# A state-space layer with its feed-forward part: y of a half in the bank of the side work, a third bank for A dt, fixed places for pieces of side work

## The chip, the cores and the metric

The kernel runs on one core of one Trainium2 chip. The metric is device time in microseconds (us) of one execution. The core's engines appear in the profile as PE (TensorE's matmuls), PEld (its weight loads), DVE (VectorE), ACT (ScalarE), POOL (GpSimd) and SP (SyncE, which issues the DMAs). Matmul results land in PSUM, a memory of eight banks of 512 f32 for each of 128 partitions.

## The reference, cut to what matters

```python
xn = x * rsqrt(mean(x * x) + 1e-6) * norm_w
xn = xn * sigmoid((xn @ select_proj_w.T + select_proj_b) * select_gate)
xp = xn @ x_proj_w.T                       # delta, B, C: 128 columns each
dt = softplus(delta @ dt_proj_w.T + dt_proj_b)
...
h = exp(dt[:, :, None] * A) * h + (dt * xt)[:, :, None] * bt[:, None, :]
y = einsum('bdn,bn->bd', h, ct)
...
x = layernorm(x + (y + x * D_param) @ out_proj_w.T)
x = layernorm(x + (silu(x @ w_gate.T) * (x @ w_up.T)) @ w_down.T)
```

There are 2 sequences of 1024 tokens, 512 channels, 128 states for each channel, and a hidden layer of 2048. All is f32.

## The kernel before

**Steps, halves, groups.** The tokens are taken in 64 *steps* of 32 tokens. A step has two *halves* of 256 channels, and a half has eight *groups* of 32 channels; so there are 1024 groups, numbered `k`, and `r = k % 8` is the place of a group in its half. For each group TensorE makes two matmuls `bu` (L705: dt x B, a tile of two banks) and two matmuls `a` (L417: A dt) for the *next* group. They use 32 rows of the array each, on four different row tiles, and are issued as bu, a, bu, a. ScalarE takes `exp` of the two `a` (L424) into `a_sb`, and VectorE runs the recurrence over the 32 tokens of the group with one scan (L726). The carried state enters at a group's first token: where the group is the first of a pair, VectorE adds it (L723), in every second group ScalarE copies it in (L713).

**y.** When a half's eight scans are done, `y_round` (L436) contracts its states with C: eight rounds of four matmuls, one round for four tokens. They run during the next half, as `ROUNDS` says: three behind group 1, three behind group 4, two behind group 7. Both halves of a step share one PSUM tile in a pool of its own (`ps_y`), and `y_out` (L449 to L452) empties it once a step: a ScalarE copy and three GpSimd operations.

**Side work.** Everything else is put between the groups by the class `Work`: `pre` (the projections of the next 256 tokens), `post` (out projection and first layer norm of 128 tokens) and `ffn`. These are Python generators. "E" asks for another engine's step (given at the top of every group by `others`), "P" begins a *piece* of TensorE work in the one bank of the pool `ps_m` (`misc`), "H" goes on with it. I call what runs between two yields a *unit*: two matmuls of 128 columns, or one of 256 columns. A piece of `gu` (gate and up), of `d` (down) or of `op` has 8 units, `sel`, `xp` and `ss` have 4, `zT`, `x1T`, `uT`, `z` have 2. A piece that has ended is emptied at the top of the next group: `gu`, `x1T` and the pieces of `pre` by ScalarE, `d` (L580), `op` (L487) and `zT` (L474) by VectorE. Until then `ps_m` holds it. `PARTS` gives credit for units behind each group: 4, 3, 3, 3, 3 behind groups 0, 2, 3, 5, 6, which is 16 in a half, and unused credit is kept up to 6.

**PSUM.** ps_y 1 bank, ps_m 1, ps_bu 2 x 2, ps_a 2: all eight. After the loop ps_bu and ps_a are released, the side work gets six banks more, and what is left of it runs alone.

Of the kernel before, what the change touches and what calls it, by code (L numbers as in the profile page):

```python
# [9 lines left out]
FP = mybir.dt.float32  # L10
# [5 lines left out]
P = 128  # L16
# [3 lines left out]

ROUNDS = ((), (0, 1, 2), (), (), (3, 4, 5), (), (), (6, 7))
PARTS = (4, 0, 3, 3, 0, 3, 3, 0)
RMS_EPS = 1e-6
# [11 lines left out]
def kernel(  # L35
# [122 lines left out]
    def misc(name):  # L158
        return bank_pool[0].tile([P, 512], FP, tag="m", name=name)
# [5 lines left out]
    def pre(c):  # L165
# [47 lines left out]
        for a in (slice(0, 2), slice(2, 4)):  # L213
# [3 lines left out]
            yield "E"  # L217
        yield "P"


        for m in range(NM):
            ps = misc(f"sel_{c}_{m}")
            yield from matmuls(ps, sel_w, m, xn)
            nc.scalar.activation(
                u[:, m, :], ps[:, 0:n], AF.Relu,
                bias=neg[:, 1, m : m + 1], scale=neg[:, 0, m : m + 1],
            )
            nc.scalar.activation(
                dt[:, m, :], ps[:, 0:n], AF.Abs, bias=gate_b[:, m : m + 1], scale=col(V_GATE, m)
            )  # L230
            yield "P" if m + 1 < NM else "E"
# [6 lines left out]
        yield "P"  # L238


        for g, dst in ((0, low), (2, c_sb)):
            ps = misc(f"xp_{c}_{g}")
            yield from matmuls(ps, xp_w, g, xn)
            nc.scalar.copy(dst, ps[:, 0:n])
            yield "P"

# [10 lines left out]
        for st in range(n_s):  # L257
# [4 lines left out]
            )  # L262
        yield "P"

        for a in range(0, NM, 2):
            ps = misc(f"z_{c}_{a}")
            for m in (a, a + 1):
                nc.tensor.matmul(  # L268
                    ps[:, ts(m - a, n)], dt_w[:, ts(m, P)], low, start=True, stop=True
                )  # L270
                yield "H" if m == a else "E"
            for m in (a, a + 1):
                z = ps[:, ts(m - a, n)]
                nc.scalar.activation(u[:, m, :], z, AF.Relu, bias=col(V_DTB, m))
                nc.scalar.activation(dt[:, m, :], z, AF.Abs, bias=col(V_DTB, m))
            yield "P" if a == 0 else "E"
        yield from softplus(dt, u)
# [4 lines left out]
        for j in range(n_j):  # L282
            yield "P"
            ps = misc(f"uT_{c}_{j}")
# [15 lines left out]
            if c == 0:  # L300
                load(0)
                diag(0, 0)
                diag(0, 1)
        yield "P"
        ps = misc(f"t0_{c}")
# [122 lines left out]
    def y_round(h, b):  # L428


        st, i = divmod(h, 2)
        if i == 0 and b == 0:
            ys[st] = ps_y.tile([P, 512], FP, tag="y", name=f"y_{st}")
        at = 28 + 28 * b
        for m in range(NM):
            nc.tensor.matmul(  # L436
                ys[st][ts(m, 32), ts(i, 256)], cz[st % 3][:, at : at + 32],
                hs[h][:, ts(m, 64), ts(b, 4)],
                start=(i == 0 and b == 0), stop=(i == 1 and b == 7),
                skip_group_check=True,  # L440
            )

    def y_out(st):

        tt, s = divmod(st, 4)
        if s == 0:
# [3 lines left out]
        nc.gpsimd.tensor_tensor(yc, yc, pick.unsqueeze(1).to_broadcast([P, P, 4]), ALU.mult)  # L450
        nc.gpsimd.tensor_tensor(yc[:, :, 0:2], yc[:, :, 0:2], yc[:, :, 2:4], ALU.add)
        nc.gpsimd.tensor_tensor(yrs[tt][:, s, :], yc[:, :, 0], yc[:, :, 1], ALU.add)  # L452
        if s == 3:
            work.add(post(tt), front=True)
# [3 lines left out]
    def post(tt):  # L458
# [6 lines left out]
        yield "E"  # L465
        yield "P"
        ps = misc(f"zT_{tt}")
# [10 lines left out]
        nc.sync.dma_start(x1, xf[tt])  # L478
        yield "P"
        ps = misc(f"op_{tt}")  # L480
# [22 lines left out]
    def ffn(tt, row):  # L503
# [24 lines left out]
        x1T = ffn_pool.tile([P, NM, P], FP, tag="x1T", name=f"x1T_{tt}")  # L528
        yield "P"
        ps = misc(f"x1T_{tt}")  # L530
# [7 lines left out]
        for what in order:  # L538
            part = int(what[1])
            if what[0] == "g":  # L540
# [3 lines left out]
                for f in range(0, NH, 2):  # L544
                    fetch(at + 4)
                    yield "P"
                    ps = misc(f"gu_{tt}_{part}_{f}")
# [20 lines left out]
            for half in range(2):  # L568
                fetch(at + 4)
                yield "P"  # L570
                ps = misc(f"d_{tt}_{part}_{half}")
# [48 lines left out]
    class Work:  # L620


        def __init__(self):
            self.gens, self.holder = [], None

# [17 lines left out]

        def tensor(self):

            if self.holder is not None:
                if self.holder[1] != "H":
                    return False
                self.step(self.holder)
                return True  # L650
            for item in self.gens:
                if item[1] == "P":
                    self.holder = item
                    self.step(item)
                    return True
            return False

        def finish(self, item):
# [21 lines left out]
    pres, begun, credit = {}, set(), 0  # L680
# [74 lines left out]
    y_out(NS - 1)  # L755
    ps_a.release()
# [8 lines left out]

    for pool in (bank_pool[0], ps_m, ps_y, hid_pool[0], ffn_pool, post_pool, main):
        pool.release()
# [67 lines left out]
```

## Time and profile before

| | |
|---|---|
| three runs | 2877.86, 2883.38 (median), 2885.7 us |
| profiled execution | 2885.05 us, span of its instructions 2882.4 us |
| first scan begins, last scan ends | 43.3 us, 2795.9 us |
| DVE busy | 2460.8 us, of which 1024 scans of 2283 ns: 2326.7 us |
| ACT busy | 1640.0 us, of which 2048 exp of 582 ns: 1084.8 us |
| POOL busy | 1838.5 us |
| granted TensorE clock, mean | 0.985 |

Busy times are sums over the whole span; a matmul row is as long as the profiler models it, and four matmuls on four row tiles can run at once, so that PE's busy time is a union and not a sum. "Idle before" names what ended an engine's idle time. The loop over the groups is nearly the whole span: it is followed by a tail of 87 us.

### The profile page before, as it was taken

Reading aid. Unit: us, or ns where it says so; the run is one execution under the profiler, and the core shown is the slowest. Engines: PE = TensorE matmul, PEld = TensorE weight load, DVE = VectorE, ACT = ScalarE, POOL = GpSimd, SP = SyncE. Lnnn points to the kernel's source line nnn. Section 1 sums busy time; section 2 is a strip of 40 time slices with the busy share of each in tenths; the row PEclk is TensorE's granted clock in tenths of the full one; section 3 lists DMA queues with packets and bytes.
Section 4 is the critical chain, followed back from the end, with each engine's and each line's share of the span. In section 5 each row is a group of like instructions: output and inputs, shape, how many; then the busy total and the mean of one; then the engine's idle time right before and its main releaser. Section 6 shows DMA issues by size and latency. Waiting matters only on the chain.

```text
span 2882.4 us, 58142 instructions
## 1 busy us (share of the span) xinstructions
PE 2781.4 (96%) x22728; PEld 1518.3 (53%) x22728; DVE 2460.8 (85%) x1680; ACT 1640.0 (57%) x3663; POOL 1838.5 (64%) x2140
## 2 busy tenths in 40 slices
PE   7989899999999999999999999999999999999998
PEld 4434454555555555455555555555555555555558
DVE  3998789899998988898998988889998899889970
ACT  4656556555665556555666556655566555555543
POOL 4666576666666666666666666566666666666643
PEclk6999999999999999999999999999999999999999
DMA  2012221324223231223312332222331332333337
GB/s 75 20 34 74 88 89 63 96 73 136 82 76 105 89 122 52 85 96 103 105 56 82 114 103 100 67 91 83 118 100 55 111 100 96 112 102 107 103 107 234
DMA packets 139166, 266.86 MB, mean 93 GB/s; under 512 B 22480, under 2 KB 76240, under 8 KB 138896
## 3 DMA queue, kind: packets, MB, share of 16 engines
q1 hardware_dynamic: 138896, 263.16, 28.5%
q8 instruction: 182, 2.98, 0.4%
q14 instruction: 88, 0.72, 0.1%
HBM read 250.39 MB, written 12.71 MB: 91 GB/s over the span
## 4 chain that ended last, share of the span: by engine, by line
PE 84%; DVE 7%; issue 3%; ACT 3%; POOL 1%; DMA 1%; SPq 0%; DVEq 0%; ACTq 0%; POOLq 0%
PE bu L705 30%; PE gu L552 17%; PE y L436 15%; PE d L574 7%; PE a L417 7%; DVE h L726 6%; PE sel L186 2%; PE op L483 2%; PE xp L186 1%; ACT a_sb L424 1%; DMA ub_d<-uT 1%; PE b L250 1%; PE ss L203 0%; PE z L268 0%; SPq L296 0%
## 5 line engine op out<-in xcount | busy, mean ns | idle before, releaser
L726 DVE TENSOR_TENSOR_SCAN h<-a_sb,bu 128x1024 f32<-128x1024 f32 x1024 | 2326.7, 2283 | 267.1 <-ACT bu L713 144.4
L424 ACT ACTIVATE a_sb<-a 128x496 f32<-128x496 f32 x2048 | 1084.8, 582 | 445.5 <-PE a L417 370.1
L417 PE MATMUL a<-ddt,a_t 32*128 32x512 f32 x4096 | 1275.7, 647 | 7.5 <-ACT a_sb L424 4.7
L705 PE MATMUL bu<-du,ub 32*128 32x512 f32 x4096 | 1224.8, 646 | 28.1 <-DVE h L726 22.7
L388 POOL TENSOR_TENSOR ddt<-dt,hot 128x512 f32<-128x512 f32 x512 | 532.8, 1048 | 291.5 <-PE a L417 291.5
L552 PEld LDWEIGHTS gu<-x1T,w 128*128 128x128 f32 x4096 | 481.9, 192 | 231.1 <-issue 175.2
L398 POOL TENSOR_TENSOR du<-ub,hot 128x512 f32<-128x512 f32 x512 | 534.8, 1048 | 38.9 <-PE a L417 35.2
L552 PE MATMUL gu<-x1T,w 128*128 128x128 f32 x4096 | 536.8, 283 | 11.0 <-ACT x1T L536 3.5
L705 PEld LDWEIGHTS bu<-du,ub 32*128 32x128 f32 x4096 | 351.5, 184 | 354.3 <-issue 209.5
L436 PE MATMUL y<-h,cz 128*32 128x256 f32 x8192 | 523.3, 384 | 1.2 <-DVE h L726 1.2
L436 PEld LDWEIGHTS y<-h,cz 128*32 128x32 f32 x8192 | 227.3, 109 | 403.2 <-issue 291.0
L713 ACT COPY bu<-cu 128x32 f32<-128x32 f32 x496 | 94.1, 190 | 578.0 <-PE a L417 514.5
L417 PEld LDWEIGHTS a<-ddt,a_t 32*128 32x128 f32 x4096 | 393.0, 185 | 47.7 <-ACT a_sb L424 28.8
L592 POOL TENSOR_SCALAR gu<-gu 128x256 f32<-128x256 f32 x128 | 108.2, 845 | 294.0 <-ACT gu L560 289.6
L574 PE MATMUL d<-w,hid 128*128 128x256 f32 x1024 | 257.1, 393 | 7.9 <-ACT t L314 3.0
L574 PEld LDWEIGHTS d<-w,hid 128*128 128x128 f32 x1024 | 184.2, 190 | 126.9 <-issue 81.6
L450 POOL TENSOR_TENSOR yc<-yc,pick 128x512 f32<-128x512 f32 x64 | 66.5, 1039 | 153.7 <-ACT yc L449 153.7
L723 DVE TENSOR_TENSOR bu<-bu,cd 128x32 f32<-128x32 f32 x496 | 92.9, 187 | 74.0 <-PE a L417 69.1
L600 POOL TENSOR_TENSOR hid<-gu,e 128x256 f32<-128x256 f32 x128 | 93.1, 728 | 65.5 <-ACT e L598 64.7
L374 POOL TENSOR_TENSOR cd<-cd,h 128x256 f32<-128x256 f32 x124 | 106.3, 857 | 39.9 <-DVE h L726 39.9
L560 ACT COPY gu<-gu 128x512 f32<-128x512 f32 x128 | 75.0, 586 | 60.3 <-PE gu L552 60.1
L593 POOL TENSOR_TENSOR gu<-gu 128x256 f32<-128x256 f32 x128 | 94.2, 736 | 10.7
(89 smaller groups left out, 1384.0 us busy)
## 6 DMA issues: line engine op xcount, KB each, us to landing
w<-in_wgu_s_dram SPq DMA_DIRECT2D x256, 512.0 KB, 4.8
w<-in_wd_s_dram SPq DMA_DIRECT2D x128, 512.0 KB, 3.8
cd<-dt_d SPq DMA_DIRECT2D x62, 256.0 KB, 3.4
ub<-ub_d SPq DMA_DIRECT2D x64, 128.0 KB, 2.0
cu<-ub_d SPq DMA_DIRECT2D x124, 64.0 KB, 4.8
ub_d<-bt SPq DMA_DIRECT2D x64, 64.0 KB, 1.7
ub_d<-uT SPq DMA_DIRECT2D x64, 64.0 KB, 1.8
zT<-in_x_q_dram SPq DMA_DIRECT2D x16, 256.0 KB
```

What stands on the lines that cost most here:

```text
L374: nc.gpsimd.tensor_tensor(cd, cd, last, ALU.mult)
L388: nc.gpsimd.tensor_tensor(ddts[j][:, m, :, :], made[lot_of[st]][0][:, a + m, toks(st)].unsqueeze(1).to_broadcast([P, 16, S]), hot[:, ts(i, ...
L398: nc.gpsimd.tensor_tensor(dus[j][:, m, :, :], uv[:, a + m, :].unsqueeze(2).to_broadcast([P, 16, S]), hot.unsqueeze(1).to_broadcast([P, 16, ...
L417: nc.tensor.matmul(ps, a_t[ts(g, 32), m, :], ddts[k // 4][ts(g, 32), m % 2, :, :], start=True, stop=True,)
L424: nc.scalar.activation(a_sb[:, k % 3, ts(b, 16), 1:], ps[:, :, 1:], AF.Exp, scale=-1.0)
L436: nc.tensor.matmul(ys[st][ts(m, 32), ts(i, 256)], cz[st % 3][:, at : at + 32], hs[h][:, ts(m, 64), ts(b, 4)], start=(i == 0 and b == 0), s ...
L552: nc.tensor.matmul(ps[:, ts(2 * a + b, P)], w[:, a, k, :], x1T[:, k, :], start=(k == 0), stop=(k == NM - 1),)
L574: nc.tensor.matmul(ps[:, 0:HD], hid[:, f, :], w[:, f % 4, :], start=(f == 0), stop=(f == NH - 1),)
L592: nc.gpsimd.tensor_scalar_max(g, g, -80.0)
L593: nc.gpsimd.tensor_tensor(gu[:, 1, :], g, gu[:, 1, :], ALU.mult)
L705: nc.tensor.matmul(bu[:, ts(b, 16), :], prepared[st][ts(g, 32), 1, :], dus[k // 4][ts(g, 32), m % 2, :, :], start=True, stop=True,)
L726: nc.vector.tensor_tensor_scan(hs[h][:, ts(r, 32), :].rearrange("p q t -> p (q t)"), a_sb[:, k % 3, :, :].rearrange("p q t -> p (q t)"), b ...
```

## The change

```diff
-ROUNDS = ((), (0, 1, 2), (), (), (3, 4, 5), (), (), (6, 7))
-PARTS = (4, 0, 3, 3, 0, 3, 3, 0)
+ROUNDS = ((), (), (0, 1, 2, 3), (4, 5, 6, 7), (), (), (), ())
+PARTS = (4, 4, 0, 0, 3, 3, 4, 4)
+ROOM = (8, 4, 0, 0, 8, 4, 4, 8)
...
-    ps_y = tc.alloc_tile_pool(name="ps_y", bufs=1, space=PSUM)
...
-        yield "P"
+        yield NM
...
         nc.gpsimd.tensor_tensor(cd, a_n, cd, ALU.mult)
-        nc.scalar.activation(cd, cd, AF.Exp, scale=-1.0)
+    def carry_exp(st):
+        if st % NSB:
+            nc.scalar.activation(carried[st][0], carried[st][0], AF.Exp, scale=-1.0)
...
-        if i == 0 and b == 0:
-            ys[st] = ps_y.tile([P, 512], FP, tag="y", name=f"y_{st}")
+        if b == 0:
+            ys[h] = misc(f"y_{h}")
...
-        yc = post_pool.tile([P, P, 4], FP, tag="yc", name=f"yc_{st}")
-        nc.scalar.copy(yc, ys.pop(st).rearrange("p (q t) -> p q t", t=4))
+        yc = post_pool.tile([P, 64, 4], FP, tag="yc", name=f"yc_{h}", bufs=2)
+        nc.scalar.copy(yc, ys.pop(h)[:, 0:256].rearrange("p (q t) -> p q t", t=4))
...
-        def tensor(self):
+        def tensor(self, room=64):
             if self.holder is not None:
                 if self.holder[1] != "H":
                     return False
+                self.left -= 1
                 self.step(self.holder)
                 return True
             for item in self.gens:
-                if item[1] == "P":
-                    self.holder = item
+                if item[1] != "E" and item[1] <= room:
+                    self.holder, self.left = item, item[1] - 1
                     self.step(item)
                     return True
             return False
+        def idle(self):
+            while self.holder is not None:
+                self.others()
+                if self.holder is not None:
+                    self.tensor()
...
-    ps_a = tc.alloc_tile_pool(name="ps_a", bufs=2, space=PSUM)
+    ps_a = tc.alloc_tile_pool(name="ps_a", bufs=3, space=PSUM)
...
         work.others()
+        if r == 4 and h:
+            y_out(h - 1)
...
-            if i == 1 and st:
-                y_out(st - 1)
...
-        if h:
+        if ROUNDS[r] and h:
+            if r == 2:
+                work.idle()
             for b in ROUNDS[r]:
                 y_round(h - 1, b)
-        credit = min(credit + PARTS[r], 6)
-        for _ in range(min(credit, 4) if PARTS[r] else 0):
-            if not work.tensor():
-                break
-            credit -= 1
+        done = 0
+        while (done < PARTS[r] or done < 4 and work.left == 1) and work.tensor(ROOM[r] - done):
+            done += 1
...
         if r == 5 and i == 0 and st + 1 < NS:
             carry_a(st + 1)
+        if r == 7 and i == 0 and st + 1 < NS:
+            carry_exp(st + 1)
+    work.idle()
```

A half's y now lies in the bank of the side work (256 columns of it): four rounds behind group 2, four behind group 3, emptied at the top of group 4, for each half on its own. The bank that this frees goes to `a`. "P" becomes a number, the units of the piece that is to begin (the other places where it stood are changed in the same way), and `ROOM` says how large a piece may begin behind which group: 8 units behind groups 0, 4 and 7, up to 4 behind 1, 5 and 6, none behind 2 and 3, where y runs. There is no credit any more. The exp of `cd`, which carries a state into the next step, moves from group 5 to group 7. ScalarE's copy of every second group's first state (L713) stays as it is.

More of the change, by code (lines that the diff above doesn't have):

```diff
@@ L217, in pre @@
             yield "E"
-        yield "P"
+        yield NM
         for m in range(NM):
@@ L230, in pre @@
             )
-            yield "P" if m + 1 < NM else "E"
+            yield NM if m + 1 < NM else "E"
         yield from softplus(dt, u)
@@ L237, in pre @@
             yield "E"
-        yield "P"
+        yield NM
         for g, dst in ((0, low), (2, c_sb)):
@@ L244, in pre @@
             nc.scalar.copy(dst, ps[:, 0:n])
-            yield "P"
+            yield NM if g == 0 else n_j
         ps = misc(f"b_{c}")
@@ L262, in pre @@
             )
-        yield "P"
+        yield 2
         for a in range(0, NM, 2):
@@ L275, in pre @@
                 nc.scalar.activation(dt[:, m, :], z, AF.Abs, bias=col(V_DTB, m))
-            yield "P" if a == 0 else "E"
+            yield 2 if a == 0 else "E"
         yield from softplus(dt, u)
@@ L282, in pre @@
         for j in range(n_j):
-            yield "P"
+            yield 2
             ps = misc(f"uT_{c}_{j}")
@@ L303, in pre @@
                 diag(0, 1)
-        yield "P"
+        yield 1
         ps = misc(f"t0_{c}")
@@ L428, in y_round @@
     def y_round(h, b):
-        st, i = divmod(h, 2)
-        if i == 0 and b == 0:
-            ys[st] = ps_y.tile([P, 512], FP, tag="y", name=f"y_{st}")
+        if b == 0:
+            ys[h] = misc(f"y_{h}")
         at = 28 + 28 * b
@@ L436, in y_round, with y_out @@
             nc.tensor.matmul(
-                ys[st][ts(m, 32), ts(i, 256)], cz[st % 3][:, at : at + 32],
+                ys[h][ts(m, 32), 0:256], cz[h // 2 % 3][:, at : at + 32],
                 hs[h][:, ts(m, 64), ts(b, 4)],
-                start=(i == 0 and b == 0), stop=(i == 1 and b == 7),
+                start=(b == 0), stop=(b == 7),
                 skip_group_check=True,
             )
-    def y_out(st):
+    def y_out(h):
+        st, i = divmod(h, 2)
         tt, s = divmod(st, 4)
-        if s == 0:
+        if s == 0 and i == 0:
             yrs[tt] = post_pool.tile([P, 4, P], FP, tag="yr", name=f"yr_{tt}")
-        yc = post_pool.tile([P, P, 4], FP, tag="yc", name=f"yc_{st}")
-        nc.scalar.copy(yc, ys.pop(st).rearrange("p (q t) -> p q t", t=4))
-        nc.gpsimd.tensor_tensor(yc, yc, pick.unsqueeze(1).to_broadcast([P, P, 4]), ALU.mult)
+        yc = post_pool.tile([P, 64, 4], FP, tag="yc", name=f"yc_{h}", bufs=2)
+        nc.scalar.copy(yc, ys.pop(h)[:, 0:256].rearrange("p (q t) -> p q t", t=4))
+        nc.gpsimd.tensor_tensor(yc, yc, pick.unsqueeze(1).to_broadcast([P, 64, 4]), ALU.mult)
         nc.gpsimd.tensor_tensor(yc[:, :, 0:2], yc[:, :, 0:2], yc[:, :, 2:4], ALU.add)
-        nc.gpsimd.tensor_tensor(yrs[tt][:, s, :], yc[:, :, 0], yc[:, :, 1], ALU.add)
-        if s == 3:
+        nc.gpsimd.tensor_tensor(yrs[tt][:, s, ts(i, 64)], yc[:, :, 0], yc[:, :, 1], ALU.add)
+        if s == 3 and i == 1:
             work.add(post(tt), front=True)
@@ L465, in post @@
         yield "E"
-        yield "P"
+        yield 2
         ps = misc(f"zT_{tt}")
@@ L478, in post @@
         nc.sync.dma_start(x1, xf[tt])
-        yield "P"
+        yield 2 * NM
         ps = misc(f"op_{tt}")
@@ L528, in ffn @@
         x1T = ffn_pool.tile([P, NM, P], FP, tag="x1T", name=f"x1T_{tt}")
-        yield "P"
+        yield 2
         ps = misc(f"x1T_{tt}")
@@ L545, in ffn @@
                     fetch(at + 4)
-                    yield "P"
+                    yield 2 * NM
                     ps = misc(f"gu_{tt}_{part}_{f}")
@@ L569, in ffn @@
                 fetch(at + 4)
-                yield "P"
+                yield NH
                 ps = misc(f"d_{tt}_{part}_{half}")
@@ L623, in __init__ @@
         def __init__(self):
-            self.gens, self.holder = [], None
+            self.gens, self.holder, self.left = [], None, 0
         def add(self, gen, front=False):
@@ L675 @@
     ps_bu = tc.alloc_tile_pool(name="ps_bu", bufs=2, space=PSUM)
-    ps_a = tc.alloc_tile_pool(name="ps_a", bufs=2, space=PSUM)
+    ps_a = tc.alloc_tile_pool(name="ps_a", bufs=3, space=PSUM)
     for b in range(2):
         decay_exp(0, b, decay_mm(0, b))
-    pres, begun, credit = {}, set(), 0
+    pres, begun = {}, set()
     for k in range(NG):
@@ L752 @@
             carry_a(st + 1)
+        if r == 7 and i == 0 and st + 1 < NS:
+            carry_exp(st + 1)
+    work.idle()
     for j in range(8):
         y_round(2 * NS - 1, j)
-    y_out(NS - 1)
+    y_out(2 * NS - 1)
     ps_a.release()
@@ L764 @@
         work.tensor()
-    for pool in (bank_pool[0], ps_m, ps_y, hid_pool[0], ffn_pool, post_pool, main):
+    for pool in (bank_pool[0], ps_m, hid_pool[0], ffn_pool, post_pool, main):
         pool.release()
```

## The prediction

> **What bounds the kernel now.** I read the page's busy shares first, then the chain of waits, then single groups in the timeline, then the list of waits.
>
> ```profile
> PE 2781.4 (96%) x22728; PEld 1518.3 (53%) x22728; DVE 2460.8 (85%) x1680; ACT 1640.0 (57%) x3663; POOL 1838.5 (64%) x2140
> PE 84%; DVE 7%; issue 3%; ACT 3%; POOL 1%; DMA 1%; SPq 0%; DVEq 0%; ACTq 0%; POOLq 0%
> ```
>
> TensorE carries the end: 84% of the chain, and busy 96%. VectorE follows close, 85%. The Trainium skill (page "Trainium Kernel Development and Optimization", Performance Expectations) says that matmul busy time is a bad metric, because matmuls are pipelined. By the row, 2882.4 - 2781.4 = 101 us is all that any new order can win. The timeline sides with the rule. Two groups (start us, length, engine, line, what; bu and a alternate):
>
> ```profile
> 1404.07 0.59 PE L705 MATMUL bu<-du,ub 32*128 32x512 f32 x1
> 1404.61 2.05 PE L552 MATMUL gu<-x1T,w 128*128 128x128 f32 x16
> 1404.90 1.05 ACT L424 ACTIVATE a_sb<-a 128x496 f32<-128x496 f32 x2
> 1406.59 0.69 PE L705 MATMUL bu<-du,ub 32*128 32x512 f32 x1
> ...
> 1416.82 0.69 PE L705 MATMUL bu<-du,ub 32*128 32x512 f32 x1
> 1417.22 0.69 PE L417 MATMUL a<-ddt,a_t 32*128 32x512 f32 x1
> 1418.27 0.71 PE L552 MATMUL gu<-x1T,w 128*128 128x128 f32 x4
> ```
>
> The group at 1403.54 has its four matmuls side by side and is done with them at 1404.61: 1.07 us. In the group at 1416.82 the last `a` begins only at 1417.22, and the side work at 1418.27, after 1.45 us. TensorE counts as busy all the while. What the late `a` waited for:
>
> ```profile
> PEld bu L705 <- DVE h L726: 42.9, 40, 1.7
> PEld a L417 <- ACT a_sb L424: 28.8, 81, 2.8
> PEld op L483 <- DVE zT L474: 13.9, 11, 1.6
> PEld d L574 <- DVE x L580: 10.0, 10, 1.4
> PEld gu L552 <- DVE x L580: 6.6, 7, 1.4
> ```
>
> The exp of the `a` before it, in the same bank. The row's 28.8 us counts only empty queues. So I compared, for every group, the end of both exps with the start of the block behind them: in some 280 of 1020 blocks an exp ends too late, and these blocks lose 161 us together, 21 of it in the first 64 groups. There the scan sets the pace (157.9 us for 64 groups, and 64 x 2.283 + 24 x 0.187 = 151 us are DVE's own), so 140 us can be had.
>
> **TensorE's own time.** Two rounds of y take 1.00 us (1415.82 to 1416.82), three 1.43 (1407.66 to 1409.09): 0.43 a round. Four units of gu take 1.98, three 1.53: 0.45 a unit. A block of bu and a takes 1.08, and whatever follows it some 0.18 once. From the order of both programs I count the units behind each group. The loop before: 2552 us by these prices, of 2752 (40.2 to 2792.2). The loop after holds 48 units more, since the tail falls from 164 to 116, but more groups have nothing behind them (151 against 55), each of which saves 0.18: 2557 us. **+5.**
>
> **A third bank for a.** Each `a` then waits for an exp one earlier. At today's exp times the 140 us would shrink to about 41. But the groups become less even. The commonest half has 4, 0, 0, 0, 3, 3, 2, 4 units, and 81 of 128 groups r = 1 are empty (75 behind the start). There the next block comes 1.11 us after its predecessor. The exps of a block with ScalarE's copy end their first at 1.89 (start 1403.54; two exps from 1404.90 to 1405.95). The second `a` of r = 2 needs just that one: it waits 1.89 - 1.11 = 0.78, say 0.8 us. The bounds: nothing, if PE is held up elsewhere; 0.97, which short blocks behind an empty group lose today on two banks. 75 x 0.8 = 60 us. I keep 20 for waits behind late ScalarE steps, half of the remaining 41. 140 becomes 80: **-60.** The scan doesn't stop PE there: bu of r = 2 needs the buffer of r = 0, whose scan ends 1.74 + 2.29 = 4.03 us after that group began, and PE arrives at 3.05 + 1.11 = 4.16. Elsewhere 36 groups behind the start are empty, two in a row as a rule, and there PE does wait for scans (about 2.0 us for a pair by the same reckoning, 36 us in all). Today's 25 such groups lose some 16 us by the same cause: **+20.**
>
> **y in the bank of the side work.** Against this change speaks a rule of the Trainium skill ("Perfetto Trace Analysis", Matmuls): independent matmul groups should rotate through different PSUM banks, so that the evacuation of one overlaps the next one's matmuls. Here y joins a queue for one bank. By the rule each of 127 halves pays two evacuations, 0.58 before y and 0.37 behind it (rows of 512 and 256 columns): 120 us. By the rows nearly none is seen: a bank filled behind one group is emptied at the top of the next, and there PE has 1.08 us of bu and a in front of its next use. The cover fails where VectorE empties it, since its scan of 2.28 us is ahead in the queue. At 1451.64 zT ends the work of its group, its addition starts at 1454.09, and op at 1454.80, 0.8 us after its block. In the order of before 36 pieces emptied by VectorE have the next user behind the very next group; after, 73: 15 zT to op, 37 d to the next piece, 21 to y. The three rows above hold 30.5 us in 28 waits, 1.09 each. For the 52 I take the same share and price, 52 x 28/36 x 1.09 = 44, for the 21 in front of y (behind two blocks of PE work) 0.3: 50 us in all, **+20.** Between zero and the longest wait shown, 1.6 us for all 73 (+86).
>
> **Other edits.** y_out: ScalarE copies 128 x 0.37 instead of 64 x 0.58, +10 us; GpSimd 128 x (0.73 + 0.46 + 0.3) against 64 x 2.07, +58 us (the rows of 256 and 128 columns; the last is an estimate from them). They lie beside TensorE's groups; ScalarE is 57% and GpSimd 64% busy. Behind the copy in ScalarE's queue wait the next exps, but y has ended by the time they become possible. Behind GpSimd's wait stand `ddt` and `du`, wanted two groups later, 5 us. Without that cover each would cost 0.4 us a half, 50 us. cd's exp two groups later has its result due a half later: nothing. SP's queue gets no new DMA. Side work of the next 256 tokens was once forced (one group of 13.2 us, 8 over its price); the new order has none: -8. But uT and t now follow in adjacent groups for all lots, and ScalarE waits for their DMAs (13.1 us in t's row today); some 1 us a lot: +8. Together **0.**
>
> **The tail.** Before, 2792.2 to 2882.4 us: 90.2. Its first part did what was left of token block 14, and the chain of the last block (y, out projection, layer norm) lay beside that:
>
> ```profile
> 2795.93 3.64 PE L436 MATMUL y<-h,cz 128*32 128x256 f32 x58 [1.18 <-DVE h L726]
> 2804.51 3.72 PE L483 MATMUL op<-out_w,zT 128*128 128x256 f32 x16 [0.85 <-DVE zT L474]
> 2808.06 14.45 PE L552 MATMUL gu<-x1T,w 128*128 128x128 f32 x128
> 2810.86 0.81 ACT L499 ACTIVATE x<-x,off_a,rstd_a 128x512 f32<-128x512 f32 x1 [0.40 <-POOL off_a L498]
> ```
>
> After, only one d is left over. The chain stands alone: from the last bu d 4.8 us, its emptying 0.6, y 3.5, yc 2.1, zT and the addition 1.7, op 3.8, layer norm 3.6: 20.1. From x1T of the last block to the end are 52.9 us today (2829.5 to 2882.4). 20.1 + 52.9 = 73: **-17.**
>
> **Sum.** +5 - 60 + 20 + 20 + 0 - 17 = -32. The profiled execution took 2885.05 us (2.65 around its span), 1.7 above the median of 2883.38. 2885 - 32 = **2853.**
>
> **Rivals.**
> 1. *The third bank does more*: PE, held up earlier in the half by another wait, reaches r = 2 later and finds its bank free, as 1.89 - 1.11 needs only 0.8 us of delay. Both remainders (60 + 20) fall away: 2773; with half, 2813. For it speaks that VectorE's queue is seldom empty; against it, that delay of PE costs the same. I put it at 2795.
> 2. *One bank becomes the stall*: each of the 73 neighbours costs the longest wait shown, 1.6 us: 117 - 30.5 = +86 instead of +20, so 2919. It decides from (50 + 32) / 73 = 1.1 us for each. For it: behind these pieces PE runs ahead of a scan that takes 2.28 us; against it: 8 of 36 such places show no wait today.
> 3. *Nothing comes of it*: where no late exp holds PE, the scan does (1023 scans and their additions need 2430 us of the loop), and the wait only changes its name: -60 becomes about -30, 2883. That the third bank isn't used is no case: three tiles rotate by construction.
>
> **Numbers.** Forecast 0.45, own range 2830 to 2876; rival 1 0.17, rival 2 0.24, rival 3 0.14. Runs of this kernel tell 0.3%, 9 us, from no change. Faster: the forecast but for its upper edge (0.43) and rival 1: 0.60. Within: rival 3's middle and that edge, 0.13. Slower: rival 2 and the rest of rival 3, 0.27. The range 2800 to 2908 leaves out the far half of rival 2 and the lower end of rival 1.
>
> **What would show it.** Right: the wait of `a` on `a_sb` survives only behind empty groups, mostly at r = 2; the last scan ends near 2781; the tail is near 73 us; DVE rises to about 86%. Wrong: more than 80 us of waits for x (L580's line) and zT ahead of d, op, x1T or y; y's matmuls waiting for ScalarE; PE's idle time above 150 us.

## The result, and the profile after

| | before | after |
|---|---|---|
| median | 2883.06 us (4 runs) | 2952.84 us (4 runs, 2945.69 to 2955.31) |
| ratio, 95% interval | | 1.024 (1.0217 to 1.0263) |
| profiled execution, its span | 2885.05, 2882.4 us | 2945.69, 2943.9 us |

The kernel is slower by 2.4%, some 70 us, where 30 us less were forecast. The page of after, its row of busy times and the first row of its chain of waits:

```profile
PE 2740.6 (93%) x22728; PEld 1467.2 (50%) x22728; DVE 2469.7 (84%) x1680; ACT 1654.3 (56%) x3727; POOL 1874.8 (64%) x2332
PE 75%; POOL 9%; DVE 8%; ACT 4%; issue 4%; DMA 1%; SPq 0%; DVEq 0%; POOLq 0%; ACTq 0%
```

PE is busy 41 us less than before, in a run that is 61 us longer. Its idle time is 203 us (2943.9 - 2740.6), twice the 101 of before, and the chain spends 75% on it, not 84%. What PE and its weight loads waited for, from the list of waits of after (engine, line, what was waited for; us in total, times, longest):

```profile
PEld a L421 <- ACT a_sb L428: 57.7, 83, 0.8
...
PEld bu L717 <- DVE h L738: 55.3, 43, 1.8
...
PE bu L717 <- DVE h L738: 47.9, 59, 1.4
...
PEld d L578 <- DVE x L584: 40.7, 23, 2.1
...
PEld op L487 <- DVE zT L478: 34.8, 16, 2.4
...
PE op L487 <- DVE zT L478: 22.2, 16, 1.5
...
PE d L578 <- DVE x L584: 21.7, 23, 1.3
```

The wait for `a_sb` is still there, with twice the sum: 83 times, none over 0.8 us, where before had 81 times and a longest of 2.8. The waits of `op` and `d` for VectorE and of `bu` for the scan (`h`) have grown. In before, PE's own rows for them are:

```profile
PE bu L705 <- DVE h L726: 22.7, 44, 1.3
...
PE op L483 <- DVE zT L474: 5.6, 7, 0.8
...
PE d L574 <- DVE x L580: 1.6, 3, 0.5
```

These rows overlap, and a stretched block of bu and a is counted as busy. So I cut the loop, from the first `bu` of each group to the first `bu` of the next, into four parts that add up. A *block* is the time from the first `bu` of a group to the end of its last bu or a. Idle time stands ahead of the side work or y behind a block, or ahead of the next `bu`. What remains is PE at side work and y. The tail is the time from the last group's `bu` on. All are sums in us over 1023 groups, from the starts and ends in the trace:

| | side work and y | blocks | idle before side work, y | idle before bu | loop | tail |
|---|---|---|---|---|---|---|
| before | 1352 | 1337 | 35 | 28 | 2752 | 90 |
| after | 1378 | 1286 | 97 | 69 | 2830 | 74 |
| change | +26 | -51 | +62 | +41 | +78 | -16 |
| forecast | +5 | -60 | +28 | +12 | -15 | -17 |

The parts are of the profiled executions here and below. That of after was 7 us under its median, so differences of parts and of medians agree to some 10 us only.

(The forecast's +28 is its 20 for y in the shared bank and 8 for uT and t. Its +12 is 20 for scans, less 8 for the forced lot.) Blocks and tail came out near the forecast. The other three columns cost 129 us where 45 had been allowed.

The granted TensorE clock has a part in this. Its mean is 0.976, where before had 0.985: it drops to half for stretches of 3.4 us and more, which take 116 us of the loop in after and 64 us in before. One such stretch of after as a window (the clock is the third number from the end), and PE in and behind it:

```profile
858.93:869.17 10.24, 8.99 (x48) 3.68 (x52) 5.71 (x4) 5.10 (x12) 6.94 (x8) 0.50 0.30 65
```

```profile
859.52 1.12 PE L287 MATMUL uT<-ident,u 128*128 128x128 f32 x4 [2.15 <-ACT uT L292]
860.57 1.22 PE L717 MATMUL bu<-du,ub 32*128 32x512 f32 x1
...
869.99 0.69 PE L717 MATMUL bu<-du,ub 32*128 32x512 f32 x1
```

A matmul of bu takes 1.22 us in it and 0.69 behind it. Between 100 and 2700 us, after has 17 such stretches, and in the 3.4 us ahead of each PE had been idle for 1.5 to 2.3 us; before has 5, behind 1.0 to 1.9 us. So idle time seems to cost a second time. From places with the same work at both clocks I estimate that half clock makes 19 us of side work and y in after, and 3 in before. That the idle time lowers the clock is read from the order of events; no run changes the clock alone.

The window of the tail of after (us; then per engine PE, PEld, DVE, ACT, POOL, SP busy us and instructions; clock, DMA share, GB/s):

```profile
2869.70:2944.00 74.30, 59.36 (x429) 52.30 (x428) 10.29 (x16) 20.50 (x45) 21.48 (x31) 0.93 0.52 181
```

74 us against a forecast of 73.

### The profile page after: what moved, and what is told of

Its sections match the earlier page's. It is cut to its first block, busy times and chain, and to the rows that moved or that the text cites. A ratio compares the mean times of both kernels' runs of the same rounds, so it can differ in the third digit from the quotient of the medians.

```text
span 2943.9 us, 58560 instructions
## 1 busy us (share of the span) xinstructions
PE 2740.6 (93%) x22728; PEld 1467.2 (50%) x22728; DVE 2469.7 (84%) x1680; ACT 1654.3 (56%) x3727; POOL 1874.8 (64%) x2332
## 4 chain that ended last, share of the span: by engine, by line
PE 75%; POOL 9%; DVE 8%; ACT 4%; issue 4%; DMA 1%; SPq 0%; DVEq 0%; POOLq 0%; ACTq 0%
PE bu L717 27%; PE gu L556 15%; PE y L439 15%; PE d L578 7%; DVE h L738 6%; PE a L421 4%; PE sel L187 2%; POOL du L402 2%; POOL ddt L392 1%; PE op L487 1%; ACT a_sb L428 1%; PE xp L187 1%; POOL dt L325 1%; DMA ub_d<-uT 1%; POOL u L280 1%
## 5 line engine op out<-in xcount | busy, mean ns | idle before, releaser
L717 PE MATMUL bu<-du,ub 32*128 32x512 f32 x4096 | 1177.8, 652 | 69.0 <-DVE h L738 47.9
L717 PEld LDWEIGHTS bu<-du,ub 32*128 32x128 f32 x4096 | 326.3, 186 | 418.2 <-issue 187.5
L439 PE MATMUL y<-h,cz 128*32 128x256 f32 x8192 | 503.0, 386 | 6.8 <-DVE x L491 3.5
L439 PEld LDWEIGHTS y<-h,cz 128*32 128x32 f32 x8192 | 242.2, 110 | 347.9 <-issue 171.1
L421 PEld LDWEIGHTS a<-ddt,a_t 32*128 32x128 f32 x4096 | 353.6, 186 | 62.3 <-ACT a_sb L428 57.7
L454 POOL TENSOR_TENSOR yc<-yc,pick 128x256 f32<-128x256 f32 x128 | 78.5, 613 | 358.3 <-ACT yc L453 358.3
```

What stands on the lines that cost most here:

```text
L421: nc.tensor.matmul(ps, a_t[ts(g, 32), m, :], ddts[k // 4][ts(g, 32), m % 2, :, :], start=True, stop=True,)
L439: nc.tensor.matmul(ys[h][ts(m, 32), 0:256], cz[h // 2 % 3][:, at : at + 32], hs[h][:, ts(m, 64), ts(b, 4)], start=(b == 0), stop=(b == 7), ...
L717: nc.tensor.matmul(bu[:, ts(b, 16), :], prepared[st][ts(g, 32), 1, :], dus[k // 4][ts(g, 32), m % 2, :, :], start=True, stop=True,)
```

## The experiments

My theory behind the result: the third bank pays what was forecast, and the new places cost more. I saw three ways for that: pieces emptied by VectorE hold the one bank, empty groups leave PE waiting for scans, and GpSimd's extra work delays `du`.

### The three parts of the change, one at a time

`e6_places_only` is after with y's own bank and two banks for `a`. So it has the new places, y_out for each half and the later exp of `cd`, and none of the change of banks:

```diff
+    ps_y = tc.alloc_tile_pool(name="ps_y", bufs=1, space=PSUM)
...
-            ys[h] = misc(f"y_{h}")
+            ys[h] = ps_y.tile([P, 512], FP, tag="y", name=f"y_{h}")
...
-    ps_a = tc.alloc_tile_pool(name="ps_a", bufs=3, space=PSUM)
+    ps_a = tc.alloc_tile_pool(name="ps_a", bufs=2, space=PSUM)
```

> The changed kernel's places for y and for the side work and its copy of y for each half, but the banks of before: a bank of its own for y, two for a. Against the kernel with two a banks and y in the side work's bank (3011 us) it tells what sharing the bank costs by itself, against the kernel before (2882 us) what the fixed places cost. Theory (the places do the harm: lumps behind groups 7, 0, 2, 3 and nothing behind group 1): 2985 to 3010 us. Rival (sharing the bank does it): 2880 to 2920 us.

`e1_two_a_banks` is after with the third bank left unused (only the last pair of lines).

> The changed kernel with two banks for a instead of three; one bank stays unused, all else is the same. Theory (the third bank works, but the empty group r = 1 makes one a of r = 2 late all the same): some 96 blocks at r = 2 lose 0.5 us more, and blocks behind groups of 2 units (r = 7, 104 of them) lose 0.4 again: 3030 to 3060 us against 2953. Rival (the third bank was worth nothing, as scans set the pace): 2945 to 2965 us.

Measured: e6 2997.52 us (ratio 1.0396, 1.0379 to 1.0414), e1 3011.04 (1.0441, 1.042 to 1.0461), which lies between its theory and its rival. From before to after there are thus three steps:

| step | time | side work and y | blocks | idle before side work, y | idle before bu | tail |
|---|---|---|---|---|---|---|
| the places (e6 less before) | +114 | +21 | +63 | +39 | +7 | -18 |
| y in the shared bank (e1 less e6) | +14 | +6 | -3 | +14 | 0 | +3 |
| the third bank (after less e1) | -58 | -2 | -111 | +9 | +34 | -1 |

The times are differences of medians. The parts are of single executions, in which the third bank is worth 69 us and not 58. Half clock takes 152 us of e6's loop and 162 of e1's, so that the steps contain the clock, which moves with the idle time.

**The places cost 114 us** (with the later exp of `cd`, which in before gains 5, see e11), twice what the third bank brings back. y in the shared bank is the small step. In e6 y has its own bank, and yet idle time before `d` is 17 us (7 in before), before `op` 15 (5), before uT and t 20 (6), before x1T 7 (1): the waits for the side work's bank come with the places. The third bank takes 111 us out of the blocks, and 43 of them come back as idle time. The list of waits of e1, to be read against that of after above, shows both:

```profile
PEld a L421 <- ACT a_sb L428: 82.7, 205, 0.8
...
PEld bu L717 <- DVE h L738: 42.3, 41, 1.7
...
PE bu L717 <- DVE h L738: 21.2, 48, 1.3
```

`a` waits 205 times here and 83 times in after. `bu` waits 21.2 us for the scan here and 47.9 in after.

### The late a behind an empty group

A block of r = 2 behind an empty r = 1, and its late `a`, in the timeline of after (start, length, engine, line, what; the bracket holds the idle time before it and what ended that):

```profile
1441.25 0.69 PE L717 MATMUL bu<-du,ub 32*128 32x512 f32 x1
...
1442.22 1.08 PE L717 MATMUL bu<-du,ub 32*128 32x512 f32 x3
1442.49 0.19 ACT L725 COPY bu<-cu 128x32 f32<-128x32 f32 x1 [0.55 <-PE a L421]
1442.62 1.05 ACT L428 ACTIVATE a_sb<-a 128x496 f32<-128x496 f32 x2
1443.25 1.12 PE L421 MATMUL a<-ddt,a_t 32*128 32x512 f32 x2
1444.30 0.42 PE L439 MATMUL y<-h,cz 128*32 128x256 f32 x4
```

The first of the two exps ends near 1443.2, and the second `a`, which needs its bank, begins at 1443.25. The block that began at 1442.22 ends at 1444.3, after 2.1 us, not 1.1. Behind the first 64 groups the blocks of r = 2 lose 82 us over 1.08 us each, nearly all of it in some 75 late ones. The forecast said 75 times 0.8 = 60. In e1 the same place loses 121 us. `e8_half_pieces` puts two units behind groups 0 and 1 where after has four and mostly none, so that a large piece is taken in two halves:

```diff
-PARTS = (4, 4, 0, 0, 3, 3, 4, 4)
+PARTS = (2, 2, 0, 0, 3, 3, 4, 4)
```

> The changed kernel with 2 and 2 units behind groups 0 and 1 in place of 4 and 4, so that a piece begun behind group 7 ends behind group 1 and group 1 is seldom empty; 72 more units are left to the tail. Theory (group 1 empty makes the second a of group 2 late, 84 us): blocks lose 60 to 75 us less, pieces emptied by VectorE right in front of y cost 25 to 40 more: 2905 to 2930 us. Rival (the late a hides a wait for the scan, which comes in its place): 2940 to 2965 us.

Measured: 2995.35 us (1.0386, 1.037 to 1.0401), slower than after by 42 us, outside theory and rival. The r = 2 blocks do lose only 22 us. But the piece now ends behind group 1 and not behind group 0, one group ahead of y, in the same bank. The list of waits of e8:

```profile
PEld y L439 <- ACT gu L564: 57.1, 63, 2.5
PEld y L439 <- DVE x L584: 48.3, 26, 1.9
...
PEld y L439 <- DVE x L491: 30.6, 15, 2.1
...
PEld a L421 <- ACT a_sb L428: 29.0, 34, 1.1
```

y's idle time rises from 6 to 66 us. In e8 the loop also takes 72 units fewer, and the tail grows to 101 us: that is half of the 52 us between the two spans.

`e4_even_places` moves y one group forward, behind groups 1 and 2, with places in every other group:

```diff
-ROUNDS = ((), (), (0, 1, 2, 3), (4, 5, 6, 7), (), (), (), ())
-PARTS = (4, 4, 0, 0, 3, 3, 4, 4)
+ROUNDS = ((), (0, 1, 2, 3), (4, 5, 6, 7), (), (), (), (), ())
+PARTS = (4, 0, 0, 3, 3, 4, 3, 3)
...
-ROOM = (8, 4, 0, 0, 8, 4, 4, 8)
+ROOM = (4, 0, 0, 8, 8, 4, 8, 8)
...
```

> The changed kernel with y behind groups 1 and 2 and the side work as 3, 3, 2 and 3, 3, 2 units behind groups 3 to 5 and 6, 7, 0, so that few groups have nothing behind them (59 under two units behind the first 64 groups, and seldom the same r; 113 units in the tail). Theory (the late a of r = 2 costs 84 us of blocks, because group 1 is empty): 55 to 80 us faster than the changed kernel, 2873 to 2898 us. Rival (the late a only stands where PE would wait for a scan anyway): within 15 us of the changed kernel.

Measured: 3009.15 us (1.0445, 1.0425 to 1.0464), outside theory and rival. Blocks fall by 53 us against after, to 1233, the least of all kernels with the full scan. Idle time ahead of side work and y doubles to 189 us, 82 of it ahead of y, 26 before op, 25 before gu, 21 before d. Side work and y take 46 us more, with half clock in 164 us of the loop (116 in after) and more and shorter runs of side work. So the empty r = 1 was what kept y and the piece before it apart: **the hole that made `a` late was the cover that y needed.** With one bank, one of the two is paid.

### Who empties the one bank

`e2_two_side_banks` is e1 with the unused bank given to the side work and y:

```diff
-    ps_m = tc.alloc_tile_pool(name="ps_m", bufs=1, space=PSUM)
+    ps_m = tc.alloc_tile_pool(name="ps_m", bufs=2, space=PSUM)
```

> As the run before it, but the bank set free goes to the side work and y, which then have two in turn. Theory (97 us of PE's idle time in front of side work and y come from the one bank that is emptied behind a scan): 70 to 80 us faster than two banks for a alone, so 2960 to 2985 us. Rival (PE waits there for data, for scans or GpSimd, and not for the bank): no more than 20 us faster than it.

Measured: 2963.1 us (1.0282, 1.0257 to 1.0308), 48 us under e1, where 70 to 80 were expected, and 10 over after. Idle time ahead of side work and y falls from 88 to 17 us, and 16 of the 17 are before `op`. Blocks grow by 25 instead: PE arrives earlier at an exp that is not done. So the second bank is worth about 48 us net, about as much there as the third at `a` (58).

A wait of `d` for the bank in the timeline of after:

```profile
1411.83 1.13 PE L578 MATMUL d<-w,hid 128*128 128x256 f32 x4
...
1412.31 2.29 DVE L738 TENSOR_TENSOR_SCAN h<-a_sb,bu 128x1024 f32<-128x1024 f32 x1
...
1413.43 0.59 PE L717 MATMUL bu<-du,ub 32*128 32x512 f32 x1
...
1414.51 0.40 DVE L584 TENSOR_TENSOR x<-x,d 128x256 f32<-128x256 f32 x1
...
1414.96 0.48 PE L578 MATMUL d<-w,hid 128*128 128x256 f32 x1 [0.93 <-DVE x L584]
```

The first `d` ends at 1412.96. VectorE began a scan at 1412.31 and comes to the addition, 0.40 us of work, only at 1414.51. PE is done with its block near 1414.02 and waits 0.93 us. In after, 22 such places take 20.8 us together, 0.95 each.

`e3_scalar_empties` has ScalarE copy zT, op and d out of the bank, and VectorE adds from the copy. `e10_scalar_empties_d` does it for `d` alone:

```diff
+    def out_of(ps, name):
+        n = ps.shape[-1]
+        t = post_pool.tile([P, D], FP, tag="ev", name=f"ev_{name}")
+        nc.scalar.copy(t[:, 0:n], ps)
+        return t[:, 0:n]
...
-                nc.vector.tensor_tensor(part_of, part_of, ps[:, 0:HD], ALU.add)
+                nc.vector.tensor_tensor(part_of, part_of, out_of(ps[:, 0:HD], f"d_{tt}_{part}_{half}"), ALU.add)
```

> The changed kernel, with d, op and zT copied out of their bank by ScalarE into SBUF, and VectorE's addition reading that copy; the bank is free as soon as the copy is done. Theory (a bank that is emptied behind a scan costs 57 us before op, d, x1T and y): 35 to 55 us faster than the changed kernel, 2898 to 2918 us. Rival (GpSimd's queue is the new bound, its share of the chain having gone from 1% to 9%): at most 10 us faster, 2943 to 2955 us.

> The changed kernel with d alone copied out by ScalarE (zT and op as they were, since copying these out too made op and t later). Theory (PE really loses the waits for d's bank): d, x1T wait 28 us less, nothing else moves, 2920 to 2932 us. Rival (VectorE's scans set the pace behind these places, so PE only arrives earlier at the next bu): less than 10 us, 2943 to 2955 us.

Measured: e3 2951.86 us (1.024, 1.0222 to 1.0259), no change from after, where 35 to 55 us were expected. e10 2923.57 (1.0146, 1.0131 to 1.0162), 29 us less than after. The lists of waits, e3 first, then e10:

```profile
PEld op L493 <- DVE zT L484: 45.5, 16, 3.3
...
PE t L308 <- ACT uT L292: 14.4, 7, 2.8
```

```profile
PEld d L584 <- ACT ev_d L465: 17.4, 23, 0.8
...
PEld x1T L542 <- ACT ev_d L465: 9.8, 13, 0.8
```

In e10 no PE row for `d` is left, only weight loads that could have run ahead (0.8 us at most, while PE is at its block): the idle time before `d` is 0.2 us (21 in after), before x1T 1.3 (8.7 in after). Of these 28 us some 8 come back before y, t and xp. The median falls by 29 us, the profiled execution by 21. In e3 the same is won and lost again. `op` needs zT's *sum*, not only its bank, and the copy puts one step more ahead of it (idle before op 20.8 to 28.7 us, before t 7 to 14, blocks +7). So of the VectorE-emptied pieces, `d` waits for the bank, and `op` for data, which agrees with e2, where `op` waits 16 us with two banks.

### GpSimd

`e9_pool_behind_diag` leaves TensorE's order as it is and moves GpSimd's three y operations behind the `ddt` and `du` of group 4:

```diff
+        ycs[h] = yc
...
+    def y_sum(h):
...
+        if r == 4 and h:
+            y_sum(h - 1)
```

> The changed kernel with the same order on TensorE; only GpSimd's three operations on y move, from in front of group 4's ddt or du to behind it. Theory (before bu PE waits mostly for scans): within 8 us of the changed kernel, 2945 to 2961 us, and the idle time before bu stays at 60 us or more. Rival (GpSimd, standing still for ScalarE's copy, makes du and ddt late): 15 to 40 us faster, idle time before bu under 45 us.

Measured: 2950.97 us (1.0237, 1.0223 to 1.0251), the same as after. GpSimd waits less for ScalarE's copy of y, 255 us in 83 places where after has 358 in 120, and PE's waits hardly move. The list of waits of e9:

```profile
PE bu L724 <- DVE h L745: 39.5, 50, 1.4
...
PE bu L724 <- POOL du L402: 13.1, 11, 1.4
...
POOL yc L463 <- ACT yc L453: 255.3, 83, 15.7
```

In after `bu` waits 47.9 us for the scan and 14.0 for `du`, this too in 11 places. Idle time before bu is 63 us against 69. So the place of the three operations costs nothing. GpSimd's share of the chain (9% in after, 1% before) is still 9% in e9, so the edit doesn't tell what the rest of GpSimd's work costs; the 14 us are all that PE's own row shows of it.

`e5_pool_later` moved those operations to the top of group 5, and ScalarE's copy stayed:

```diff
+        if r == 5 and h:
+            y_sum(h - 1)
```

> The changed kernel; ScalarE's copy of y stays at the top of group 4, the three GpSimd operations on it come at the top of group 5, so that GpSimd's queue no longer stands still for the copy (358 us of waiting in the changed kernel). Theory (GpSimd's late du and ddt make about 20 us of PE's waits before bu, the scans the rest): 5 to 20 us faster than the changed kernel, 2933 to 2948 us. Rival (GpSimd is the new bound): 40 us faster or more.

Measured: 2976.12 us (1.0326, 1.0304 to 1.0349), slower, against theory and rival. This says nothing on GpSimd. `post` is added there too, a group later, and misses its places: 98 units more are left to the tail, which grows from 74 to 116 us. That is more than the whole difference of 23.

### What the scan takes

`e13_after_half_scan` and `e14_before_half_scan` are after and before with the scan over 512 of a group's 1024 columns. Half of the states aren't computed; y and GpSimd's product of the carried states read the other half twice. All else stays:

```diff
...
-            hs[h][:, ts(r, 32), :].rearrange("p q t -> p (q t)"),
-            a_sb[:, k % 3, :, :].rearrange("p q t -> p (q t)"),
-            bu.rearrange("p q t -> p (q t)"),
+            hs[h][:, ts(r, 16), :].rearrange("p q t -> p (q t)"),
+            a_sb[:, k % 3, 8:24, :].rearrange("p q t -> p (q t)"),
+            bu[:, 8:24, :].rearrange("p q t -> p (q t)"),
```

> The changed kernel with every scan over 512 of the 1024 columns (half of the states aren't computed, y reads the other half twice; TensorE's and ScalarE's work is the same). Theory (scans stand behind the idle time before bu, 69 us, behind the bank emptied by VectorE, 57 us, and set the pace of the first 64 groups): 95 to 135 us faster, 2815 to 2858 us. Rival (ScalarE's exps and PE's own order set these waits): less than 40 us faster, above 2912 us.

> The kernel before with the same shorter scan. Theory (it loses only 28 us before bu and some 15 behind VectorE's emptying to the scans, and the first 64 groups): 45 to 75 us faster, 2808 to 2838 us, so that the changed kernel's distance of 70 us shrinks to 0 to 30. Rival: less than 25 us faster, the distance stays above 50 us.

Measured: a scan takes 1220 ns instead of 2283. After falls by 120 us, to 2832.74 (0.9819, 0.9805 to 0.9833), before by 19, to 2864.34 (0.9935, 0.9923 to 0.9948). **With a short scan the changed kernel is the faster one, by 32 us.** That this is also the size of the gain forecast is chance: the forecast was for the full scan. Busy times and chain of e13:

```profile
PE 2732.6 (97%) x22728; PEld 1486.7 (53%) x22728; DVE 1404.7 (50%) x1680; ACT 1649.4 (58%) x3727; POOL 1872.1 (66%) x2332
PE 86%; POOL 7%; ACT 4%; issue 1%; DMA 1%; SPq 0%; DVE 0%; ACTq 0%; POOLq 0%; DVEq 0%
```

VectorE has left the chain, and PE's idle time is 99 us. In the parts: idle before bu 69 to 0.4 us, before `op`, `d` and x1T 50 to 3, side work and y 40 us less, blocks 32 more. Half clock takes 45 us of the loop, not 116, an estimated 14 of the 40. The first 64 groups, which have nothing but scans to wait for, take 126 us instead of 159. GpSimd still has 7% of the chain, though `bu` waits for nothing: a share of the chain alone is no loss. That the blocks of r = 2 lose 89 us here too shows that the late `a` has nothing to do with the scan.

In before the first 64 groups gain only 3 us (158 to 155), and blocks grow by 37: on two banks the exps bind as soon as the scan lets go. My expectation of e14 (45 to 75 us faster) missed this.

### Before with single edits

`e7_y_spread` is before with one round of y behind nearly each group:

```diff
-ROUNDS = ((), (0, 1, 2), (), (), (3, 4, 5), (), (), (6, 7))
-PARTS = (4, 0, 3, 3, 0, 3, 3, 0)
+ROUNDS = ((), (0,), (1,), (2,), (3,), (4,), (5,), (6, 7))
+PARTS = (3, 2, 2, 2, 2, 2, 2, 1)
```

> The kernel before, with y spread over the half: one round behind each of groups 1 to 6, two behind group 7, and credit for 3, 2, 2, 2, 2, 2, 2, 1 units of side work; the banks are those of before. Theory (uneven groups make a late, and 140 us are lost by it before): most groups then last about 2.5 us, longer than the exps take, so blocks lose some 100 us less; pieces emptied by VectorE have their next user one group later more often, which gives back 30 to 50: 2815 to 2850 us. Rival (TensorE's time goes elsewhere as soon as a wait is taken away, since scan and TensorE are both near their limits): 2870 to 2900 us.

Measured: 2962.15 us (1.0274, 1.0256 to 1.0291), slower, where theory said faster. Blocks fall by 55 us and idle time barely moves, so even groups do what was hoped of them. But side work and y take 151 us more. 52 units more (some 23 us) explain a part only; see the last section.

`e11_cd_exp_later` is before with only the exp of `cd` moved from group 5 to group 7, as after has it:

> The kernel before with one part of the change alone: the exp of cd two groups later. Theory: ScalarE no longer waits for GpSimd's product in front of the exps of group 6, some 0.2 us in each of 64 steps: 5 to 15 us faster, 2868 to 2878 us. Rival (all of it hidden): within 3 us of before.

Measured: 2878.56 us (0.9982, 0.9975 to 0.9988), faster than both kernels by little. The loop falls by 8 us, 7 of it ahead of side work and y. `e15_cd_exp_and_scalar_d` adds the ScalarE copy of `d` to it:

> The kernel before with the two edits that helped: the exp of cd two groups later, and d copied out of its bank by ScalarE. Theory (d's bank costs before only 7 us in front of d and part of 9 in front of gu): 5 to 12 us faster than with the exp alone, 2866 to 2874 us. Rival (ScalarE's 64 copies more make exps late there, where a has only two banks): 2878 to 2890 us.

Measured: 2878.54 us (0.9985, 0.9978 to 0.9991). Nothing is added, where 5 to 12 us were expected: in before `d` waits only 6.6 us.

`e12_even_group_7` is e11 with a unit behind group 7, whose two rounds of y leave the block of r = 0 short of time on two banks:

```diff
-PARTS = (4, 0, 3, 3, 0, 3, 3, 0)
+PARTS = (4, 0, 3, 3, 0, 3, 3, 1)
```

> The kernel of the run before it with one unit of side work behind group 7 too, which has two rounds of y and lasts only 2.1 us, so that the exps of group 0 come late in 77 of 120 halves. Theory (uneven groups make a late; a unit costs no more there than elsewhere, plus 0.14 us for a change of the tile's shape): block time falls by some 35 us, net time rises by 15: 2845 to 2868 us. Rival (as with y spread over all groups, changes of shape eat it): 2875 to 2900 us.

Measured: 2915.13 us (1.0112, 1.0098 to 1.0126), slower than theory and rival. The blocks of r = 0 lose 10 us instead of 45, as expected. Yet those of r = 1, 3, 4 and 6 lose some 40 us more together, and 52 units move from the tail into the loop (+44 us of side work and y, tail -19). A late `a` that is removed at one place comes back at the next.

## Why the prediction was wrong

- **What bounds the kernel**: right for before, half right for after. TensorE's busy time fell by 41 us and the time rose by 61, which sides with the rule of the Trainium skill that the prediction weighed ("Trainium Kernel Development and Optimization", Performance Expectations: matmul busy time is a bad metric). VectorE, 85% busy, was taken as an engine that follows. Its scans are the second bound: e13 gives 120 us.
- **"TensorE's own time +5"**: +26. The 48 units cost what was said (22 us). A place left empty does save, though less than the 0.18 us of the forecast: at the full clock two, three and four rounds of y take 0.93, 1.36 and 1.80 us, which is 0.43 a round and 0.07 once, and by the same differences a run of `gu` has 0.13. Fewer runs of y save 9 us, blocks with nothing behind them, which run on into the next, 8, and 29 more runs of side work take back 4. What is left, some 16 us by estimate, is the half clock (19 us in after, 3 in before), for which the prediction had no term.
- **Third bank, -60**: -51, near but flattering. 13 of the 51 lie in the first 64 groups, where the scan sets the pace and 12 us come back as idle time before bu; behind them blocks fall by 38. The remainder of 0.8 us at r = 2 was right in place, count (75) and nearly in size (82 us for 60).
- **Empty groups waiting for scans, +20**: with the forced lot +12 was forecast, and +41 came, 12 of it in the first 64 groups. I asked at each place only whether the scan before it ends in time (4.03 against 4.16 us at r = 2). A margin of 0.1 us doesn't last: behind the first 64 groups `bu` of r = 2 waits 13 us in all in after (7 in e6), and `bu` of r = 0 14 (none in before). With the third bank PE runs ahead until the next thing stops it, and that is the buffer of `bu`, which has two tiles as before: after less e1 is +34 in this column. The half scan takes it to 0.4.
- **y in the shared bank, +20, with uT and t +28**: +62. For after the reckoning was good: by starts and ends PE is idle there for VectorE's emptying in 15 places of `op` (20.8 us), 22 of `d` (20.8), 13 of `x1T` (7.4), 15 of y (3.6) and one of `zT` (0.9), 53 us, and 50 were forecast. The 30.5 us taken off for before were wrong. They are rows of weight loads, which can be held up while PE is still at its block; PE's own idle time behind VectorE in before is 12 us. So the term should have been +41. uT and t take 16 us for the 8 given to them, and sel 6 that had no term. Sharing itself costs 14 (e1 less e6): e6, with a bank for y alone, has 39 of the 53 us, from pieces that the *places* put close behind one another. The Trainium skill's rule that independent groups should rotate through banks ("Perfetto Trace Analysis", Matmuls) would, with the prices of the prediction, have charged 120 us to y, and y waits for 6.
- **Other edits at nothing**: right for y's three operations at GpSimd (e9). ScalarE's copies weren't tried alone. The exp of `cd`, two groups later, is no cost but a gain of 5 us, at least in before (e11).
- **Tail, -17**: -16.
- **The rivals and the signs.** None of the three rivals is what happened. Rival 2 had the right sign and one of the right causes, but put all of it on the one bank, while two banks there (e2) take out only 48 us. Rival 3 named the right mechanism, *where no late exp holds PE, the scan does*, but took it for a bound on the gain. It comes on top of the places, which cost 114 us by themselves. Two of the prediction's signs of being wrong came: the rows for x (L584 in after) and zT ahead of d, op, x1T and y hold some 100 us, more than 80, and PE is idle for 203 us, more than 150.

The steps that failed are thus three terms of the sum: the waits of today that were taken off the one-bank term (30.5 us where PE loses 12), the waits of `bu` for scans (+12, measured +41), and TensorE's own time (+5, measured +26). Behind the last two lies one habit, a sum over single places, each priced with all others at rest.

What stays open: e13 shortens both what `bu` waits for and what `d` and `op` wait for, and takes most of the half clock with it, so its 120 us aren't split between these; e10 shows 21 to 29 of them for `d`. Three tiles of `bu` next to three banks for `a` and one for the side work would need ten banks of eight, and weren't tried.

## What to carry to other kernels

When three engines take turns within a few per cent of each other, a buffer added on one edge moves the wait to the next one: look up which buffer stops the faster engine next, and count what it stops there. An idle slot in an order may be the cover of something else, so change places of work one at a time and before the buffers. When you take a wait of today off a forecast, take the idle time of the engine itself, and not that of loads which could run ahead. And a long in-order instruction (here the scan) on the engine that frees a shared bank costs what remains of it, not what the freeing costs: give such pieces to the engine with short ones, where only the bank is waited for and not the data.

## What the runs showed of the hardware that was not expected

A run of equal matmuls costs PE a fixed time besides its matmuls, going from y (weights 128 x 32) to side work (128 x 128) costs some more, and PE's rows count both as work. Medians at the full clock, of PE's time behind a block, from e7: two rounds of y alone take 0.93 us, one unit of gu alone 0.57, and the two together 1.57, which is 0.07 more than their sum. With the 0.07 of a run of y and the 0.13 of a run of gu from above this is an account of e7's 151 us, as an estimate: 508 more runs of y (35 us), 318 more runs of side work (40), 793 more changes from y to side work within a place (54), and 52 units (23), 152 us in all. The list of waits, in which "issue" is time with nothing to wait for, shows it at y's weight loads in e7 (before has 291.0 us in 385 places, with the same longest of 1.5):

```profile
PEld y L436 <- issue: 676.2, 892, 1.5
```

And the row of busy times of e7 calls it all work, 97% busy, which once more can't tell a stretched run from a full one:

```profile
PE 2859.9 (97%) x22728; PEld 1427.9 (48%) x22728; DVE 2477.5 (84%) x1680; ACT 1639.3 (55%) x3663; POOL 1837.6 (62%) x2140
```

No run changes one of these costs alone. The clock is no rival here: in e7 half clock takes 37 us of the loop, less than in before.
